# A four-layer graph network on one core: one tile fewer for ScalarE in each step's first group, and one place moved between two buffers

## The chip, the cores and the metric

The kernel runs on one core of a Trainium2 chip. A core has five engines, each with a queue of its own: TensorE (PE, with its weight loads shown as PEld), VectorE (DVE), ScalarE (ACT), GpSimd (POOL) and SyncE (SP), which here only issues transfers (DMAs). They wait for each other by semaphores. The metric is the time of one execution on the device in microseconds (us), as the median of several runs.

## The reference

The reference runs four graph layers one after the other on x (3327 x 256) with one adjacency matrix adj (3327 x 3327, about 1% of it set, plus the diagonal). Each layer normalises x, applies a ReLU and adds its result to x. What matters here is layer 0:

```python
R = S + jnp.eye(N); R = R / R.sum(-1, keepdims=True)       # S is adj
for n in range(2):                                         # two steps
    A = _top_p_attention(Xa, W1, W2, W3)
    Xf = R @ Xf
    Xa = A @ Xa
    Z = Z + Xf @ U1[n].T + Xa @ U2[n].T
```

`_top_p_attention` computes q k^T, a softmax over each row, and keeps in each row the largest probabilities until their sum reaches 0.9; the rest is set to zero and the row is divided by what was kept. Layers 1 to 3 (a sum over neighbours with tanh weights, and two attentions masked by adj) follow and are not touched.

## The kernel before

Rows are handled in 26 tiles of 128 (the last has 127). Layer 0 has two steps (s = 0 and 1), and each step handles the tiles in nine groups of three (`FG`; the last has two). All data are 32-bit floats.

**A group** (`group`, L996) goes through these stages:

- For each tile, q is loaded, PE makes the scores (L1037), DVE moves them from PSUM into the tile's buffer e with the row maxima (`evicted`, L1011), and ACT takes the exponential with the row sum (L1020). There are six buffers for e.
- A first guess of each row's threshold is made, with one DVE pass over half of each tile (L1080).
- Four rounds (`ROUNDS`, L1110) narrow the threshold. A round needs, for each tile, the sum of the entries at or above the row's threshold. DVE gets it in one pass (L1126). ACT needs two passes, a ReLU and a sign (L1121), from which DVE combines the sum (L1132, L1133). `ON_ACT` = [2, 2, 1, 2] says how many of the group's tiles ACT takes in each round; the rest are DVE's. Short DVE instructions on 128x3 values (L1136 to L1153) then move the threshold, and the next round needs the new one: ACT gets it negated (L1114).
- For each tile, DVE finds the exact cut with three passes (L1168, L1171, L1182) and appends the weighted sum to the list of other work.

**The other work** of a step, called generators in the code, is advanced beside the groups:

- `neighbours` (L898) is R @ Xf for one tile. It loads the tile's column of adj in four parts into `blk` (three places, L905). In step 0 ACT also writes the signs of each part into `sg` (L908), which go to memory for the later layers (L909). POOL adds the identity to the diagonal block (L912), after the sign was taken. PE sums 26 products in 52 matmuls in the one PSUM place of `ps_acc` (L914). ACT scales the row (`xf_row`, L922), after DVE's reciprocal of the row sum in step 0 (L920), and the row is stored (L923).
- `weighted` (L926) is A @ Xa and the update of Z for one tile. It loads the stored row into `xf_in` (L934), and in step 1 the row of Z so far into `base_row` (L932, one place). PE transposes e (L950), ACT copies it to `wt` (L952), PE sums the products (L940), and ACT scales the result (`xa` or `xa_row`, L962). Then that row and `xf_in` are transposed (L785, copied by L786) and multiplied by U1 and U2 (L970). DVE adds the row of Z (L978).

**The order of the work.** `overlapped` (L1191) starts a group every 20 ticks and advances all generators by one part each tick. This gives the program's order. Tile, the framework below it, lays down the order on each engine's queue before the run: it takes the program's order as priority and lets work go ahead whose inputs and buffers it expects to be free. So neighbour sums of later groups run ahead in the first group's rounds, before there is weighted work. Buffers come from pools: tiles with the same tag share `bufs` places, and a new tile waits until a place is free. `sg` and `xf_in` are from the pool `f0t`, whose default is two places (L1319). All transfers named here go through SP's queue.

Of the kernel before, what the change touches and what calls it, by code (L numbers as in the profile page):

```python
# [9 lines left out]
F32 = mybir.dt.float32  # L10
# [3 lines left out]
I8 = mybir.dt.int8  # L14
# [6 lines left out]
P = 128  # L21
# [4 lines left out]
D = 256  # L26
# [8 lines left out]
ON_ACT = [2, 2, 1, 2]  # L35
# [26 lines left out]
def rows_of(it):  # L62
    return P if it < NT - 1 else LAST
# [3 lines left out]
def kernel(  # L67
# [678 lines left out]
    def layers(fast):  # L746
# [9 lines left out]
        def ps_wide():  # L756
            return psf.tile([P, 2 * 512], F32, tag="wide", bufs=2, name="ps_wide")

        def ps_acc():
            return psf.tile([P, 512], F32, tag="acc", name="ps_acc0")  # L760

        def ps_out0():
            return psf.tile([P, 512], F32, tag="out", name="ps_out0")

        def ps_row():
            return psf.tile([P, 512], F32, tag="row", bufs=2, name="ps_row")
# [11 lines left out]
        def rows_to_load(it):  # L778
            return LAST_ROWS if it == NT - 1 else [(0, P)]
# [20 lines left out]
        def layer0(wp, mp, ap_, tp, sp):  # L800
            def turned(src, tag, bufs):
                t = tp.tile([P, 2, P], F32, tag=tag, bufs=bufs, name=tag)
                transposed(src, t.rearrange("p c r -> p (c r)"))
                return t
# [47 lines left out]
            def keys_of(xt, s, it):  # L852

                ps = ps_row()
                f, i = divmod(it, HB)
                for c in range(2):
                    nc.tensor.matmul(ps[:, :P], wkq[:, f, c, :], xt[:, c, :], start=(c == 0), stop=(c == 1))
                b, o = f * DA, (1 - f) * DA
                r = rows_of(it)
                nc.scalar.activation(  # L860
                    kt[b : b + DA, s, i * P : i * P + r], ps[b : b + DA, :r], AF.Copy,
                    accum_out=key_sums[b : b + DA, s, i : i + 1],
                )
                qs = tp.tile([P, P], F32, tag="qs", name="qs")
                nc.scalar.copy(qs[o : o + DA, :], ps[o : o + DA, :P])
                nc.sync.dma_start(q_d[s, it], qs[o : o + DA, :])
# [31 lines left out]
            def neighbours(s, it, xf):  # L898

                acc = ps_acc()  # L900
                w = XW if s == 0 else D
                for chunks in QB:
                    n = len(chunks)
                    blk = ap_.tile([P, 7, P], F32, tag="blk", name="blk")
                    nc.sync.dma_start(blk[:, :n, :], adj_t[it, :, chunks[0] : chunks[0] + n, :])  # L905
                    if s == 0:
                        sg = tp.tile([P, 7, P], I8, tag="sg", bufs=1, name="sg")
                        nc.scalar.activation(sg[:, :n, :], blk[:, :n, :], AF.Sign)  # L908
                        nc.sync.dma_start(sign_d[it, :, chunks[0] : chunks[0] + n, :], sg[:, :n, :])  # L909
                    if it in chunks:  # L910
                        j = it - chunks[0]
                        nc.gpsimd.tensor_tensor(blk[:, j, :], blk[:, j, :], ident, ALU.add)  # L912
                    for j, jc in enumerate(chunks):
                        nc.tensor.matmul(  # L914
                            acc[:, :w], blk[:, j, :], xf(jc)[:, :w], start=(jc == 0), stop=(jc == NT - 1)
                        )
                    yield
                yield
                if s == 0:
                    nc.vector.reciprocal(rr[:, it : it + 1], acc[:, D : D + 1])  # L920
                row = tp.tile([P, D], F32, tag="xf_row", name="xf_row")
                nc.scalar.mul(row, acc[:, :D], rr[:, it : it + 1])  # L922
                nc.sync.dma_start((xf_d, xf2_d)[s][it * P : (it + 1) * P, :], row)  # L923
                yield

            def weighted(s, it, e, norm, xa, xa_next, us):  # L926

                if s == 0:
                    base = h(it)[:, :D]
                else:  # L930
                    base = tp.tile([P, D], F32, tag="base", bufs=1, name="base_row")
                    nc.sync.dma_start(base, zz_d[it * P : (it + 1) * P, :])  # L932
                xf_in = tp.tile([P, D], F32, tag="xf_in", name="xf_in")
                nc.sync.dma_start(xf_in, (xf_d, xf2_d)[s][it * P : (it + 1) * P, :])  # L934
                po = ps_out0()[:, :D]

                def products(wt, j0, m):
                    for k in range(m):
                        jc = j0 + k
                        nc.tensor.matmul(  # L940
                            po, wt[:, k * P : (k + 1) * P], xa(jc)[:, :D], start=(jc == 0), stop=(jc == NT - 1)
                        )

                ready = None
                for j0 in range(0, NT, 8):
                    m = min(8, NT - j0)
                    pt = ps_wide()
                    for k in range(m):
                        jc = j0 + k
                        nc.tensor.transpose(pt[:, k * P : (k + 1) * P], e[:, jc * P : (jc + 1) * P], ident)  # L950
                    wt = tp.tile([P, 8 * P], F32, tag="wt", name="wt")
                    nc.scalar.copy(wt[:, : m * P], pt[:, : m * P])  # L952
                    if ready:
                        products(*ready)
                    ready = wt, j0, m
                    yield
                products(*ready)
                if s == 0:
                    row = xa_next(it)[:, :D]
                else:  # L960
                    row = tp.tile([P, D], F32, tag="xa_row", bufs=1, name="xa_row")
                nc.scalar.mul(row, po, norm)  # L962
                yield
                xt = turned(row, "xt", 2)
                xft = turned(xf_in, "xft", 2)
                yield
                pz = ps_row()
                for n, (lhs, u) in enumerate(((xft, us[0]), (xt, us[1]))):
                    for cc in range(2):
                        nc.tensor.matmul(  # L970
                            pz[:, :D], lhs[:, cc, :], u[:, cc, :],
                            start=(n == 0 and cc == 0), stop=(n == 1 and cc == 1),
                        )
                if s == 0:
                    keys_of(xt, 1, it)
                yield
                zrow = tp.tile([P, D], F32, tag="zrow", bufs=1, name="zrow")
                nc.vector.tensor_tensor(zrow, pz[:, :D], base, ALU.add)  # L978
                nc.sync.dma_start(zz_d[it * P : (it + 1) * P, :], zrow)
                yield  # L980
                if s == 0:

                    xb = tp.tile([P, D], F32, tag="xa_row", bufs=1, name="xb")
                    r = rows_of(it)
                    for a, b in rows_to_load(it):
                        nc.sync.dma_start(xb[a:b], x[it * P + a : it * P + b])
                    nc.gpsimd.tensor_tensor(xb[:r], xb[:r], b_b[:r], ALU.add)
                    nc.sync.dma_start(xb_d[it * P : it * P + r, :], xb[:r])
# [7 lines left out]
            def group(s, tiles, xa, xf, xa_next, us, slots, products_of, also):  # L996


                g = len(tiles)
# [108 lines left out]
                todo = list(products_of)  # L1108
                first = 2 if g == len(todo) else 0
                for r in range(ROUNDS):  # L1110
                    on_act = list(range(max(g - ON_ACT[r], g - 2 if g > 2 else 1), g)) if g > 1 else []
                    A = slice(on_act[0], g) if on_act else None
                    if on_act:
                        nc.scalar.mul(minus[:, 0, A], v[:, 3, A], -1.0)  # L1114
                    if r >= first and todo:
                        also.append(neighbours(s, todo.pop(0), xf))
# [74 lines left out]
            def overlapped(makers, apart, later=(), when=None):  # L1191
# [5 lines left out]
                while makers or running or also or waiting:  # L1197
# [15 lines left out]
            overlapped(  # L1213
                [
                    lambda also, t=t: group(0, t, h, h, xa1, us0, lambda it: e_slot(it % 6), t, also)
                    for t in groups
                ],
# [42 lines left out]
            def entered(it):  # L1260
# [29 lines left out]
                for c in range(2):  # L1290
# [6 lines left out]
            overlapped(  # L1297
                [
                    lambda also, t=t: group(
                        1, t, xa1, lambda jc: xf[jc // HB][:, jc % HB, :], None, us1, slots,  # L1300
                        products_of(t), also,
# [13 lines left out]
        with ExitStack() as l0:  # L1315
# [3 lines left out]
            tp = l0.enter_context(tc.tile_pool(name="f0t", bufs=2, reuse_waits="tile"))  # L1319
# [127 lines left out]
        with tc.tile_pool(name="l1", bufs=2, reuse_waits="tile") as l1:  # L1447
# [15 lines left out]
            for it in range(NT):  # L1463
# [20 lines left out]
                r = rows_of(it)  # L1484
# [244 lines left out]
```

## Time and profile before

| | us |
|---|---|
| median of 3 runs | 3117.26 |
| lowest and highest | 3114.98, 3118.21 |
| the profiled execution's own time | 3111.67 |
| its span, first to last instruction | 3109.9 |
| first x row of step 0 scaled (L962) | 216.6 |
| last of step 0 | 1016.7 |
| first x row of step 1 scaled (L962) | 1149.5 |
| last of step 1 | 1998.3 |

The mean granted TensorE clock was 0.973 of full speed. In what follows, "busy" is time in which an engine executes; a row of the stretches gives the start and end, the length, and the busy time of PE, PEld, DVE, ACT and POOL with the number of instructions, then the granted clock, the share of the DMA engines and GB/s. A row of an engine's timeline gives start, duration, engine, line, operation, output and inputs, and in brackets how long the engine was idle before it and what ended that. A row of the waits names who waited for whom, the total, the number of times and the longest. The page's group rows give the busy time, the mean duration in ns and the idle time before.

### The profile page before, as it was taken

To read this page: it belongs to the slowest core of one execution; us is meant where nothing else is said; L and a number is where in the kernel's file an instruction comes from. 1 tells how busy PE (TensorE), PEld (TensorE's weight loads), DVE (VectorE), ACT (ScalarE), POOL (GpSimd) and SP (SyncE) were. 2 spreads that over 40 slices of the span, in tenths; PEclk is the share of its full clock that TensorE was granted. 3 is DMA by queue.
4 is the path that set the end of the run, shared out by engine and by line. 5 is a ranking of instruction groups with operands and counts; after the bars stand their busy time and mean duration, and the time that the engine had idled before them with its cause. 6 is when DMAs were issued, how large, how long until landed. Compare 5 with 4: busy or idle time off the path is not lost. (4 is left out here: it accounts for less than half of the span.)

```text
span 3109.9 us, 37662 instructions
## 1 busy us (share of the span) xinstructions
PE 2831.8 (91%) x13454; PEld 2278.7 (73%) x13454; DVE 2382.5 (77%) x4159; ACT 1968.2 (63%) x2607; POOL 375.5 (12%) x716
## 2 busy tenths in 40 slices
PE   7788899999999899999999988999997999979998
PEld 5466677777778577767777767788876787758887
DVE  3678888778873588888976868577765999769996
ACT  6767787768763666677665645333334776757776
POOL 0220010000001000000000014311120233210000
PEclk9899999999999999999999999999998999989999
DMA  4431112331242232211232232388861211112221
GB/s 137 131 102 51 55 42 77 91 89 49 70 119 88 76 97 60 59 43 51 73 89 79 76 110 75 111 315 313 321 228 33 71 59 57 31 49 78 72 76 38
DMA packets 183034, 298.83 MB, mean 96 GB/s; under 512 B 24700, under 2 KB 137015, under 8 KB 179511
## 3 DMA queue, kind: packets, MB, share of 16 engines
q1 hardware_dynamic: 182838, 296.34, 30.3%
q8 instruction: 108, 1.77, 0.2%
q14 instruction: 88, 0.72, 0.1%
HBM read 251.97 MB, written 44.30 MB: 95 GB/s over the span
## 5 line engine op out<-in xcount | busy, mean ns | idle before, releaser
L1121 ACT ACTIVATE junk_a<-e,minus 128x3328 int8<-128x3328 f32 x208 | 638.7, 3071 | 3.7
L1588 PE MATMUL ps_wide<-wh,places 128*128 128x257 f32 x1872 | 452.5, 384 | 35.9 <-DVE places L1582 34.8
L1588 PEld LDWEIGHTS ps_wide<-wh,places 128*128 128x128 f32 x1872 | 354.4, 192 | 94.5 <-ACT places L1580 16.5
L914 PE MATMUL ps_acc<-h,blk 128*128 128x258 f32 x1352 | 333.6, 399 | 44.5 <-ACT xf_row L922 35.3
L1011 DVE TENSOR_SCALAR_CACHE_REDUCE e<-ps_wide 128x1024 f32<-128x1024 f32 (+1 forms) x176 | 178.4, 1019 | 212.0 <-PE ps_wide L1037 211.5
L914 PEld LDWEIGHTS ps_acc<-h,blk 128*128 128x128 f32 x1352 | 262.1, 199 | 99.9 <-ACT xf_row L922 40.5
L914 PE MATMUL ps_acc<-xf,blk 128*128 128x256 f32 x1352 | 314.0, 384 | 13.0 <-ACT xf_row L922 13.0
L940 PE MATMUL ps_out<-h,wt 128*128 128x256 f32 x1352 | 312.6, 383 | 5.0 <-ACT wt L952 4.9
L940 PE MATMUL ps_out<-xa,wt 128*128 128x256 f32 x1352 | 312.6, 381 | 1.4 <-ACT wt L952 1.4
L1579 ACT ACTIVATE places<-places,sd 128x512 f32<-128x512 f32 (+1 forms) x364 | 246.6, 685 | 105.5 <-PE ps_wide L1588 72.3
L1476 PE MATMUL ps_wide<-gw,blk 128*128 128x256 f32 x1352 | 303.9, 382 | 0.2 <-ACT blk L1473 0.2
L914 PEld LDWEIGHTS ps_acc<-xf,blk 128*128 128x128 f32 x1352 | 254.1, 191 | 63.2 <-ACT xf_row L922 18.5
L1476 PEld LDWEIGHTS ps_wide<-gw,blk 128*128 128x128 f32 x1352 | 257.0, 192 | 35.1 <-ACT blk L1473 0.6
L940 PEld LDWEIGHTS ps_out<-h,wt 128*128 128x128 f32 x1352 | 250.8, 191 | 41.1 <-ACT wt L952 7.0
L940 PEld LDWEIGHTS ps_out<-xa,wt 128*128 128x128 f32 x1352 | 248.3, 190 | 34.9 <-ACT wt L952 3.7
L1126 DVE SCALAR_TENSOR_TENSOR below<-e,v 128x3328 f32<-128x3328 f32 x72 | 265.4, 3687 | 1.8
L1580 ACT ACTIVATE places<-places,d 128x512 f32<-128x512 f32 (+1 forms) x364 | 235.9, 682 | 46.1 <-DVE places L1581 45.7
L1581 DVE TENSOR_TENSOR places<-places,places 128x1024 f32<-128x1024 f32 (+1 forms) x182 | 210.4, 1164 | 67.8 <-ACT places L1579 65.8
L952 ACT COPY wt<-ps_wide 128x1024 f32<-128x1024 f32 x208 | 175.1, 846 | 88.1 <-PE ps_wide L950 87.4
L1037 PE MATMUL ps_wide<-keys,q 64*128 64x512 f32 (+1 forms) x832 | 214.8, 567 | 16.0 <-DVE e L1011 13.1
L1582 DVE SCALAR_TENSOR_TENSOR places<-blk_s,places 128x1024 f32<-128x1024 int8 (+1 forms) x182 | 206.1, 1141 | 2.0
L1020 ACT ACTIVATE e<-e,nm 128x3327 f32<-128x3327 f32 x44 | 134.8, 3064 | 85.3 <-DVE nm L1019 85.2
(274 smaller groups left out, 4314.8 us busy)
## 6 DMA issues: line engine op xcount, KB each, us to landing
blk<-in_adj_t SPq DMA_DIRECT2D x104, 448.0 KB, 3.4
blk<-in_adj_t SPq DMA_DIRECT2D x52, 832.0 KB, 6.8
adj_rows<-in_adj SPq DMA_DIRECT2D x25, 1663.5 KB, 8.1
blk<-in_adj_t SPq DMA_DIRECT2D x104, 384.0 KB, 3.3
blk_s<-sign_d SPq DMA_DIRECT2D x72, 256.0 KB, 2.9
blk_s<-pos_d SPq DMA_DIRECT2D x44, 416.0 KB, 3.6
pos_d<-pos SPq DMA_DIRECT2D x22, 416.0 KB, 2.8
xf_d<-xf_row SPq DMA_DIRECT2D x52, 128.0 KB, 2.4
```

The source lines that it names most:

```text
L914: nc.tensor.matmul(acc[:, :w], blk[:, j, :], xf(jc)[:, :w], start=(jc == 0), stop=(jc == NT - 1))
L940: nc.tensor.matmul(po, wt[:, k * P : (k + 1) * P], xa(jc)[:, :D], start=(jc == 0), stop=(jc == NT - 1))
L1011: nc.vector.tensor_scalar(e.rearrange("p (f c) -> p f c", f=2)[:, :, c0 : c0 + cw], pl.rearrange("p (f c) -> p f c", f=2)[:, :, :cw], 1.0, ...
L1037: nc.tensor.matmul(pl[:, f * 512 : f * 512 + cw], q[f * DA : (f + 1) * DA, :], kt[f * DA : (f + 1) * DA, s, c0 : c0 + cw], start=True, sto ...
L1121: nc.scalar.activation(junk, es[i], (AF.Relu, AF.Sign)[n], bias=minus[:, 0, i : i + 1], accum_out=(ga, sa)[n][:, 0, i : i + 1],)
L1126: nc.vector.scalar_tensor_tensor(below, es[i], v[:, 3, i : i + 1], es[i], ALU.is_ge, ALU.mult, accum_out=v[:, 1, i : i + 1],)
L1476: nc.tensor.matmul(po, filt[:, j * P : (j + 1) * P], gw(jc), start=(jc == 0), stop=(jc == NT - 1))
L1579: nc.scalar.activation(e1[:, :, q, :], s0, AF.Exp, bias=sd[:, jc + q, 1:2])
L1580: nc.scalar.activation(e2[:, :, q, :], s1, AF.Exp, bias=d2[:, jc + q : jc + q + 1])
L1581: nc.vector.tensor_tensor(e1, e1, e2, ALU.max)
L1582: nc.vector.scalar_tensor_tensor(e1, signs[:, :n, j : j + 2, :], 0.0, e1, ALU.is_gt, ALU.min)
L1588: nc.tensor.matmul(pos_[k], e1[:, k, q, :], wh(jc + q)[:, : D + 1], start=(jc + q == 0), stop=(eye and jc + q == NT - 1),)
```

## The change

Three lines change, all in layer 0:

- `sg` has two places instead of one (its `bufs=1` goes, and the pool's two hold).
- `xf_in` has one place instead of two.
- In the rounds, the number of tiles for ACT is 1 for the group that begins with tile 0, in both steps, and `ON_ACT[r]` otherwise. In that group of three, rounds 0, 1 and 3 thus have one tile on ACT and two on DVE; round 2 has that already.

```diff
-                        sg = tp.tile([P, 7, P], I8, tag="sg", bufs=1, name="sg")
+                        sg = tp.tile([P, 7, P], I8, tag="sg", name="sg")
...
-                xf_in = tp.tile([P, D], F32, tag="xf_in", name="xf_in")
+                xf_in = tp.tile([P, D], F32, tag="xf_in", bufs=1, name="xf_in")
...
                 for r in range(ROUNDS):
-                    on_act = list(range(max(g - ON_ACT[r], g - 2 if g > 2 else 1), g)) if g > 1 else []
+
+                    most = 1 if tiles[0] == 0 else ON_ACT[r]
+                    on_act = list(range(max(g - most, g - 2 if g > 2 else 1), g)) if g > 1 else []
                     A = slice(on_act[0], g) if on_act else None
```

## The prediction

> **What bounds the kernel now.** I read the engine totals first, then layer 0 cut into stretches, then the queues of ScalarE (ACT) and VectorE (DVE) in the rounds that the change touches, then the waits. Totals, and the two kinds of pass over a tile that change engines:
>
> ```profile
> PE 2831.8 (91%) x13454; PEld 2278.7 (73%) x13454; DVE 2382.5 (77%) x4159; ACT 1968.2 (63%) x2607; POOL 375.5 (12%) x716
> ...
> L1121 ACT ACTIVATE junk_a<-e,minus 128x3328 int8<-128x3328 f32 x208 | 638.7, 3071 | 3.7
> ...
> L1126 DVE SCALAR_TENSOR_TENSOR below<-e,v 128x3328 f32<-128x3328 f32 x72 | 265.4, 3687 | 1.8
> ```
>
> One tile in one round costs ACT two passes of 3.07 us, 3.26 us apart with the accumulator's read (6.5 us), or DVE one pass of 3.69 us (3.77 with its read).
>
> The stretches: step 0's fill, two periods of its groups, a full period; step 1's fill and a period after it.
>
> ```profile
> 75.00:210.00 135.00, 101.62 (x404) 72.59 (x403) 93.58 (x199) 92.24 (x81) 36.94 (x46) 0.87 0.47 135
> 1025.00:1132.00 107.00, 95.20 (x411) 69.17 (x410) 74.70 (x173) 65.88 (x50) 11.22 (x23) 0.97 0.40 110
> ...
> 216.00:305.00 89.00, 78.97 (x389) 60.10 (x387) 75.70 (x147) 68.09 (x73) 2.22 (x14) 0.96 0.14 40
> 305.00:402.00 97.00, 87.71 (x424) 67.31 (x424) 84.53 (x165) 75.95 (x80) 5.58 (x19) 0.96 0.18 53
> 504.00:608.00 104.00, 98.33 (x491) 77.08 (x489) 82.40 (x159) 78.56 (x84) 3.38 (x18) 1.00 0.26 76
> 1149.00:1238.00 89.00, 82.48 (x407) 62.85 (x405) 76.85 (x149) 63.23 (x60) 4.83 (x15) 1.00 0.19 53
> ```
>
> After the length come PE, PEld, DVE, ACT and POOL busy. A full period has PE busy 98 of 104 us: TensorE (PE) bounds it. The fill has 33 us of idle PE in 135, and a clock of 0.87. The two periods behind it have 10 and 9 us idle. Step 1's fill has only 12 in 107.
>
> Why the fill is slow shows on DVE in step 0's second round, and on ACT in the same one:
>
> ```profile
> 130.74 3.69 DVE L1126 SCALAR_TENSOR_TENSOR below<-e,v 128x3328 f32<-128x3328 f32 x1
> 134.35 0.08 DVE L1126 DVE_READ_ACCUMULATOR below<-e,v 128x1 f32 x1
> 134.35 0.68 DVE L1148 SCALAR_TENSOR_TENSOR a<-v 128x3 f32<-128x3 f32 x1
> 145.80 0.16 DVE L1132 SCALAR_TENSOR_TENSOR sa<-sa,v 128x2 f32<-128x2 f32 x1 [10.77 <-ACT junk_a L1121]
> ```
>
> ```profile
> 131.04 3.07 ACT L1121 ACTIVATE junk_a<-e,minus 128x3328 int8<-128x3328 f32 x1
> ...
> 134.10 0.93 ACT L908 ACTIVATE sg<-blk 128x896 int8<-128x896 f32 x1
> 134.94 3.05 ACT L1121 ACTIVATE junk_a<-e,minus 128x3328 int8<-128x3328 f32 x1
> ```
>
> DVE does its one tile, then waits 10.77 us while ACT does four passes with signs between them.
>
> **What the Trainium skill says.** Its page "TensorE: Matmul & The Clock Gate", section Specifications, says ScalarE and VectorE run strict queues. The trace agrees: the sign at 134.10 begins only where the pass of 131.04 ends. The same page ("Part 1: The HAM clock gate") says that idle windows throttle PE: the granted clock in the fill, by stretches of 15 us, is 0.66 (150 to 165) to 1.00. The Trainium skill's page "SBUF — State Buffer", section "SBUF: two separate sides", says a DVE instruction with two SBUF inputs and a reading GpSimd (POOL) instruction exclude each other for their whole length. The trace agrees: the identity's addition to a block (L912), 0.46 us at the median, took 3.28 us at 190.48, under a DVE pass. Six more DVE passes can lengthen six such additions.
>
> **Part 1, the rounds.** Three of four rounds (0, 1, 3; round 2 already has one tile on ACT) in both steps lose one tile on ACT: 12 passes of 3.26 = 39 us of ACT work gone, 6 passes of 3.77 = 23 us of DVE work added. Per round in step 0: ACT now has 13.0 us of passes plus one to four signs of 0.9; afterwards 6.5 plus signs; DVE has 7.5 instead of 3.8, into the gap of 10.77. The round shrinks by 6.5 where ACT still ends last. Rounds 0, 1 and 3 now run from 106.5 to 130.7, 130.7 to 148.0 and 157.9 to 175.1, all ended by ACT: 3 x 6.5 = 19.5 us. In step 1 there are no signs, so DVE's 7.5 ends last: 13.0 - 7.5 = 5.5, times three is 16.5 us. Queued behind the second DVE pass are the evictions of the next group's scores (1.2 us each, for PE and the exponentials) and the reciprocal ahead of xf_row (L920), without which PE can't reuse the one ps_acc place. Each can come up to 3.8 us later; on ACT the same xf_row stands behind fewer passes. I take these as even.
>
> What of it reaches the end? PE isn't empty in these rounds: it runs the neighbour sums of later tiles ahead. One is 52 matmuls in about 11.5 us; in step 0 they come every 15 to 26 us between 115 and 190. If weighted work begins 19.5 us sooner, about one neighbour sum fewer stands behind it, and 11.5 us are owed. So step 0 gains at least 19.5 - 11.5 = 8, at most 19.5, as far as the 19 idle us of the next two periods take the debt up. I take a third of it: 12 us. In step 1 PE is idle in 12 of 107 us during the fill, so a shorter fill saves about 16.5 x 0.12 = 2 us, at most 16.5. The periods after it have only 6 to 7% idle; I take 3.
>
> **Part 2, two places for sg.** A sign now waits for the store of the one before it:
>
> ```profile
> ACT sg L908 <- DMA sign_d<-sg: 21.3, 7, 4.5
> ...
> SPq L934 <- PE ps_row L785: 139.0, 28, 17.7
> ```
>
> The first row is the fill's, the second the whole run's. Over the rest of step 0 it is another 30.9 us in 16 waits. Most delay ACT when it has nothing else. Two matter: 4.2 us at 107 in round 0, and 4.5 us at 199.8, where the copies of the first weighted tile queue behind a sign and PE idles 4.5 us. The gain is 0 to 8.7 us; some of it dies with the rounds anyway. I take 2.
>
> **Part 3, one place for xf_in.** A tile's load (L934, 2.0 us to landing) can then start only after PE has transposed the tile before (L785). It is used at the end of that tile's own products, at least 17.1 us later (the closest starts of L785 are 1000.8 and 1017.9). With two places the load already waits on this line in SP's queue, 139 us in 28 waits, because it is issued as soon as a place frees; PE's waits for a landing xf_in are nil. Behind SP's wait stand block loads and sign stores; the blocks' three places have covered that so far (PE waited once for a block, 0.8 us, in step 0's fill). base_row, which has one place in step 1, already lives so. I cost it at 2 us, between 0 and 10 for a few late ones; a gain is excluded, as a place is only taken away. If the cover is gone, a late load stops PE for about 2.5 us (issue 0.3, landing 2.0).
>
> **Sum**, against the profiled execution of 3111.7 us (span 3109.9): -12 - 3 - 2 + 2 = -15, so 3096.7. The median of the runs is 5.6 above that execution, so I expect 3102 for the median.
>
> **Rivals.**
> - *PE is the bound and only postpones* (same). The debt is paid in full: -8 - 2, no gain from sg, and xf_in costs 5: -5, 3112. For it: 98 of 104 us busy. Against it: the 19 idle us right behind the fill.
> - *The whole latency passes* (faster still). 19.5 + 16.5 + 4.5 = 40, 3077. For it: the pipeline's six tile places tie each group's scores to the weighted work two groups before, so an early start may carry on. Against it: step 1's dense PE.
> - *xf_in comes late* (slower). Place: SP's queue, where the load stands behind a block load that waits for PE to release ps_acc's operands; the longest such wait is 18.0 us, as long as the shortest spacing of the uses. Price 2.5 us for each late tile. It decides above 21 us, that is from 9 late tiles of 50: with 12, 3102 - 2 + 30 = 3130. For it: the order on the queues is fixed before the run, so a misjudged place repeats. Against it: no PE wait for it today.
>
> **Chances.** Forecast 0.47, whole latency 0.13, postponed 0.20, late xf_in 0.20. About 0.2% (6.2 us) is what a measurement of this kernel can tell from no change, so: faster 0.60, same 0.20, slower 0.20. The forecast's own range, from -6.5 to -28, is 3089 to 3111. The range over the cases, 3084 to 3125, leaves out half of the fast rival and a little over half of the slow one.
>
> **What would show it.** In the changed trace: 196 passes of L1121 instead of 208 on e (with e_h, 228 instead of 240), 94 of L1126 instead of 88; in step 0's second round a DVE wait for ACT of about 2 us instead of 10.8; the first xa row (L962) near 197 instead of 216.6, and step 1's near 1120 instead of 1149; the waits of sg for sign_d gone; no PE wait for xf_in. Step 0 should end some 12 us sooner and the rest keep its length. Wrong if the first xa row is early but step 0 ends as before (postponed), or if PE waits before L785 for a load (late).

## The result, and the profile after

| | before | changed |
|---|---|---|
| median of 8 runs each, us | 3117.74 | 3108.18 |
| lowest and highest, us | 3112.79, 3121.76 | 3102.82, 3112.04 |
| the profiled execution's own time, us | 3111.67 | 3102.82 |
| its span, us | 3109.9 | 3101.0 |
| first and last x row (L962) of step 0, us | 216.58, 1016.73 | 201.44, 1011.34 |
| first and last x row (L962) of step 1, us | 1149.46, 1998.31 | 1128.47, 1989.72 |

The changed kernel takes 0.9966 of the time of the kernel before, with a 95% interval of 0.9955 to 0.9977: 9.6 us less by the medians, 8.9 by the spans. The forecast was 15 us less, 3102 for the median. The direction and the range were right; the size was half as large again as it should have been.

From L1111 on the changed kernel's lines lie two further down: L1121, L1126, L1132 and L1168 of the kernel before are now L1123, L1128, L1134 and L1170. The page's totals and its rows for the two kinds of pass:

```profile
PE 2831.4 (91%) x13454; PEld 2280.4 (74%) x13454; DVE 2406.0 (78%) x4171; ACT 1932.2 (62%) x2583; POOL 393.2 (13%) x716
...
L1123 ACT ACTIVATE junk_a<-e,minus 128x3328 int8<-128x3328 f32 x196 | 602.0, 3071 | 4.0
...
L1128 DVE SCALAR_TENSOR_TENSOR below<-e,v 128x3328 f32<-128x3328 f32 x78 | 287.9, 3692 | 1.8
```

ACT has lost 12 passes (208 to 196) and DVE has gained six (72 to 78 on e). PE has the same work, 2831 us. The gain is therefore idle PE time that is gone, and the question is where.

DVE's timeline in the second round of step 0, where the kernel before had a wait of 10.77 us:

```profile
123.20 3.69 DVE L1128 SCALAR_TENSOR_TENSOR below<-e,v 128x3328 f32<-128x3328 f32 x1
...
127.22 3.67 DVE L1128 SCALAR_TENSOR_TENSOR below<-e,v 128x3328 f32<-128x3328 f32 x1
...
131.42 0.15 DVE L920 RECIPROCAL rr<-ps_acc 128x1 f32<-128x1 f32 x1
...
132.70 0.15 DVE L1134 SCALAR_TENSOR_TENSOR sa<-sa,v 128x1 f32<-128x1 f32 x1
```

Two passes stand where one pass and the wait stood, and the instruction that combines ACT's sum has no wait in brackets: ACT was done before it. From the first pass on e (L1126, now L1128) of round 0 to the tile stage (L1170) the first group now takes 48.05 us in step 0, from 109.01 to 157.06, and took 68.5 before: 20.5 us less. In step 1 it is 42.5 instead of 58.6: 16.1 us less.

How much of this remains shows in the stretches (columns as before). The first rows are step 0's fill and its next three periods, then step 1's fill and its next three. The periods lie between the same tiles as before. The first row can't be compared with the prediction's row of the fill, which ends 6.6 us ahead of the first x row; this one ends 1.4 us ahead:

```profile
75.00:200.00 125.00, 93.91 (x369) 65.59 (x369) 107.39 (x210) 76.97 (x70) 44.63 (x43) 0.86 0.40 121
200.00:285.00 85.00, 76.59 (x385) 58.83 (x383) 73.06 (x145) 65.23 (x71) 3.02 (x15) 0.98 0.16 45
285.00:392.00 107.00, 99.76 (x490) 77.38 (x490) 89.94 (x169) 82.41 (x86) 3.22 (x19) 1.00 0.25 72
392.00:496.00 104.00, 99.21 (x482) 77.29 (x481) 82.82 (x162) 78.45 (x84) 5.12 (x18) 0.98 0.27 77
1020.00:1111.00 91.00, 80.58 (x346) 57.01 (x347) 84.04 (x179) 46.88 (x37) 10.20 (x22) 0.96 0.38 103
1128.00:1217.00 89.00, 82.42 (x405) 62.49 (x403) 76.78 (x149) 62.89 (x59) 4.25 (x15) 1.00 0.19 51
1217.00:1315.00 98.00, 89.90 (x425) 69.04 (x426) 86.30 (x163) 69.70 (x66) 3.56 (x19) 0.95 0.20 58
1315.00:1415.00 100.00, 96.89 (x480) 76.05 (x479) 82.83 (x167) 67.14 (x64) 13.49 (x18) 1.00 0.24 70
```

Three rows of the kernel before that the prediction doesn't show: step 0's third period, and step 1's second and third.

```profile
402.00:504.00 102.00, 95.60 (x478) 74.38 (x477) 83.40 (x164) 77.38 (x84) 8.19 (x17) 1.00 0.26 76
...
1238.00:1330.00 92.00, 86.32 (x422) 65.57 (x420) 80.92 (x156) 66.28 (x62) 4.71 (x17) 1.00 0.20 56
1330.00:1423.00 93.00, 87.08 (x424) 66.25 (x424) 81.89 (x156) 66.62 (x64) 3.68 (x17) 1.00 0.19 55
```

In the changed kernel's rows, the third is the one to look at. The second period of step 0 took 97 us with PE busy 87.7 in the kernel before; now it takes 107 with PE busy 99.8 in 490 matmul records instead of 424. It holds the neighbour sum that no longer fitted into the fill. The rows scaled by `xf_row` (L922) say the same: six neighbour sums ended in the fill before (at 70, 114, 129, 155, 175 and 190 us), five now (68, 108, 132, 157 and 184). Between the x rows of tiles 3 and 6 two ended before (370 and 386), and three now (343, 364 and 384).

How much of the shorter fill was idle PE time shows from 75 us to the first x row of step 0, first before and then in the changed kernel:

```profile
75.00:216.58 141.58, 108.20 (x435) 78.32 (x434) 95.65 (x201) 98.82 (x87) 36.94 (x46) 0.88 0.45 129
```

```profile
75.00:201.44 126.44, 95.35 (x376) 66.82 (x376) 108.71 (x220) 77.06 (x70) 44.63 (x43) 0.87 0.40 120
```

The fill is 15.1 us shorter, but PE is also busy 12.9 us less in it. Only 2.3 us of what went was idle time; the rest is work that has to be done later. In the next two periods PE's idle time (length less busy time) falls from 19.3 to 15.7 us, so these take up 3.7 us of it without getting longer.

The lead of the changed kernel at successive groups' x rows in step 0 is 15.1, 20.2, 10.6, 7.8, 7.3, 7.1, 6.0 and 5.4 us, and 5.4 at the last row. The 5 us won in the first period and the 5 us lost after the second weren't traced; half of the 20.2 us goes in the second period.

In step 1 the lead is 21.0 at the first row (15.6 of it new), 21.0, 15.0, 8.1 and 8.6, and 8.6 at the last row: step 1 keeps 3.2 of its own. It pays in the same way. Five neighbour sums ended in its fill instead of six, and one in its first period instead of two. The second and third periods have three sums each, where they had two, and grew from 92 to 98 and from 93 to 100 us. Here too the shorter fill (107 to 91 us in the rows above) was nearly all PE work: PE's idle time in it fell only from 11.8 to 10.4 us.

The waits also moved. These two rows are the whole run of the kernel before, for a sign:

```profile
ACT sg L908 <- DMA blk<-in_adj_t: 57.9, 25, 8.4
...
ACT sg L908 <- DMA sign_d<-sg: 52.2, 23, 4.5
```

And in the changed kernel, with the wait of SP's queue for the place of `xf_in`:

```profile
ACT sg L908 <- DMA blk<-in_adj_t: 108.6, 40, 12.0
...
ACT sg L908 <- DMA sign_d<-sg: 4.1, 2, 2.4
...
SPq L934 <- PE ps_row L785: 189.1, 38, 22.4
```

The waits for the store of the sign before are nearly gone, 52.2 to 4.1 us, and the waits for the block itself have grown by 50.7 us. SP's waits for the place of `xf_in` grew from 139.0 to 189.1 us, yet PE never waits for a load of `xf_in`.

### The profile page after: what moved, and what is told of

The parts are those of the page before. It is cut to its first block, busy times and chain, and to the rows that moved or that the text cites. A ratio compares the mean times of both kernels' runs of the same rounds, so it can differ in the third digit from the quotient of the medians.

```text
span 3101.0 us, 37657 instructions
## 1 busy us (share of the span) xinstructions
PE 2831.4 (91%) x13454; PEld 2280.4 (74%) x13454; DVE 2406.0 (78%) x4171; ACT 1932.2 (62%) x2583; POOL 393.2 (13%) x716
## 5 line engine op out<-in xcount | busy, mean ns | idle before, releaser
L1123 ACT ACTIVATE junk_a<-e,minus 128x3328 int8<-128x3328 f32 x196 | 602.0, 3071 | 4.0
L1590 PEld LDWEIGHTS ps_wide<-wh,places 128*128 128x128 f32 x1872 | 353.8, 191 | 93.7 <-ACT places L1582 16.5
L914 PEld LDWEIGHTS ps_acc<-xf,blk 128*128 128x128 f32 x1352 | 253.9, 191 | 58.1 <-ACT xf_row L922 12.7
L1128 DVE SCALAR_TENSOR_TENSOR below<-e,v 128x3328 f32<-128x3328 f32 x78 | 287.9, 3692 | 1.8
L1037 PE MATMUL ps_wide<-keys,q 64*128 64x512 f32 (+1 forms) x832 | 215.0, 574 | 15.3 <-DVE e L1011 9.1
L1173 DVE MAX8 w<-below 128x8 f32<-128x3328 f32 x52 | 188.4, 3623 | 0.4
```

The costliest lines, as they stand in the source:

```text
L914: nc.tensor.matmul(acc[:, :w], blk[:, j, :], xf(jc)[:, :w], start=(jc == 0), stop=(jc == NT - 1))
L1037: nc.tensor.matmul(pl[:, f * 512 : f * 512 + cw], q[f * DA : (f + 1) * DA, :], kt[f * DA : (f + 1) * DA, s, c0 : c0 + cw], start=True, sto ...
L1123: nc.scalar.activation(junk, es[i], (AF.Relu, AF.Sign)[n], bias=minus[:, 0, i : i + 1], accum_out=(ga, sa)[n][:, 0, i : i + 1],)
L1128: nc.vector.scalar_tensor_tensor(below, es[i], v[:, 3, i : i + 1], es[i], ALU.is_ge, ALU.mult, accum_out=v[:, 1, i : i + 1],)
L1173: nc.vector.max(w9[:, i, 1:9], below)
L1590: nc.tensor.matmul(pos_[k], e1[:, k, q, :], wh(jc + q)[:, : D + 1], start=(jc + q == 0), stop=(eye and jc + q == NT - 1),)
```

## The experiments

The theory under test (A): the shorter rounds are a true head start, but PE had used the old, long fill to run neighbour sums ahead. A shorter fill holds one of them less, and that one is paid later, in a period that PE already fills. Against it stand: that the places of `sg` bring or cost something (sg, xf_in), that the start is lost for another reason than PE's load, and that late blocks in the fill, behind other transfers, decide. The leads below come from one profiled execution each; two kernels that should be alike there differ by up to 3 us. The last row of step 0 is at 1016.73 us before, and at 1015.63 and 1014.76 with changed places alone; it is at 1011.34 in the changed kernel, and at 1014.20 in one that differs from it in step 1 only. So smaller differences are not read, and the 3.2 us that step 1 keeps above are themselves no larger than this.

**Which part carries it.** Four kernels on one chip, with the kernel before at 3115.14 us.

The rounds alone, with the places as before:

```diff
-                    on_act = list(range(max(g - ON_ACT[r], g - 2 if g > 2 else 1), g)) if g > 1 else []
+                    on_act = list(range(max(g - (1 if tiles[0] == 0 else ON_ACT[r]), g - 2 if g > 2 else 1), g)) if g > 1 else []
```

> Only the rounds are changed (one tile on ACT in the first group of both steps); sg keeps one place and xf_in two. Theory A (the rounds carry the gain): first xa row of step 0 near 202 to 206, of step 1 some 19 us earlier than before, and 6 to 10 us less at the end (ratio 0.997 to 0.998). Rival B (the gain comes from the second place of sg, which unties ACT from the stores): ratio 0.999 to 1.001 here.

Measured: 3107.63 us, a ratio of 0.9971 (0.9960 to 0.9981), 7.5 us less. The rounds carry the gain; the lead at the first x row is 16.6 us (the row is at 199.9, earlier than expected) and at the last row of step 0 it is 3.3.

Both places alone, with the rounds as before:

```diff
-                        sg = tp.tile([P, 7, P], I8, tag="sg", bufs=1, name="sg")
+                        sg = tp.tile([P, 7, P], I8, tag="sg", name="sg")
...
-                xf_in = tp.tile([P, D], F32, tag="xf_in", name="xf_in")
+                xf_in = tp.tile([P, D], F32, tag="xf_in", bufs=1, name="xf_in")
```

> Only the buffers are changed (sg two places, xf_in one); the rounds are those of before. Theory A: within 3 us of before (ratio 0.999 to 1.001), first xa row of step 0 at 212 to 217. Rival B: 7 to 10 us less (0.997 to 0.998).

Measured: 3113.06 us, 0.9996 (0.9988 to 1.0004): no difference. The first x row came at 219.8 us, not at 212 to 217, so that part of the expectation failed. The waits of this kernel, whole run:

```profile
ACT sg L908 <- DMA blk<-in_adj_t: 92.1, 44, 6.9
...
ACT sg L908 <- DMA sign_d<-sg: 1.7, 1, 1.7
```

Without any change in the rounds, the store's 52.2 us of waits fell to 1.7 and the block load's rose from 57.9 to 92.1. A second place for the result only let ACT arrive sooner at an operand that wasn't there.

One place for `xf_in` alone:

```diff
-                xf_in = tp.tile([P, D], F32, tag="xf_in", name="xf_in")
+                xf_in = tp.tile([P, D], F32, tag="xf_in", bufs=1, name="xf_in")
```

> Only xf_in has one place; sg keeps one. Theory A: no PE wait for a load of xf_in and a ratio of 0.999 to 1.001. Rival C (the single place costs, and hides a larger gain of the other parts): 3 to 8 us more (1.001 to 1.0025), with PE idle before L785 for a load.

Measured: 3112.79 us, 0.9993 (0.9985 to 1.0001). Taking the place away costs nothing, and in this kernel too PE has no wait for a load of `xf_in`. The slow rival is refuted. Since both places together give 0.9996, the second place for `sg` is worth nothing measurable either. It was not tried alone.

The changed kernel with the new rounds in step 0 only:

```diff
-                    most = 1 if tiles[0] == 0 else ON_ACT[r]
+                    most = 1 if tiles[0] == 0 and s == 0 else ON_ACT[r]
```

> As the changed kernel, but in step 1 the first group keeps ON_ACT. Theory A: step 0 as in the changed kernel (its last xa row near 1011), step 1 as before, so 5 to 6 us less than before (ratio 0.998). If step 1 carried most of the gain instead: 1 to 2 us less (0.9995).

Measured: 3109.56 us, 0.9983 (0.9972 to 0.9993), 5.6 us less, as theory A expected. By the medians, step 0 brings a little over half of the 9.6 us and step 1 the rest; the intervals of this kernel and the changed one overlap, so the split is rough. The profiled execution, 3 us above this kernel's median, shows less: 2.5 us of lead at the last row of step 0 (at 1014.20, not near 1011) and 0.7 at that of step 1 (1997.65 against 1998.31).

The payback is the same in both kernels with new rounds above. From 75 us to the first x row the fill is 16.6 us shorter with the rounds alone and 13.9 with step 0 only, and PE is busy 16.0 and 16.8 us less in it. Five sums ended there instead of six, the second period has three instead of two, and takes 106.4 and 107.2 us instead of 97.4.

**Is it PE's load?** If PE's debt eats the head start, PE with slack must let it through. In both kernels 12 of the 26 products of each neighbour sum are left out (every second one but the last, so the sums are not the reference's):

```diff
                     for j, jc in enumerate(chunks):
+                        if jc % 2 and jc != NT - 1:
+                            continue
```

> The kernel before with 14 of the 26 products of each neighbour sum (the odd ones but the last are left out, in both steps), so PE has some 5 us less per sum, about 270 us in all; loads, signs and everything else stay. It serves as the base for the next run. Both theories: clearly faster than before, by 100 us or more (ratio below 0.97), with DVE and latency the bound in place of PE.

> The changed kernel with the same 12 products of each neighbour sum left out. Theory A (the head start of the first group is paid back because PE postpones neighbour sums and is full afterwards): with a PE that isn't full the head start survives to the end of each step, so this run is 20 to 35 us below the halved kernel of before. Rival D (the head start dies for another reason, the six places of e or DVE): it is 5 to 12 us below, as with full sums.

Measured, with the kernel before at 3113.79 us: 2997.88 (0.9631, 0.9617 to 0.9645) and 2969.61 (0.9538, 0.9525 to 0.9551). The change is now worth 28.3 us, three times as much. In step 1 the theory holds in full: 17.8 us gained at the first x row and 17.9 at the last. Eight sums ended in its fill instead of ten, and the other two came in the sixth period, which took 91.7 us with three sums in it and 93.7 with one in the kernel before: where PE had room, they cost nothing. In step 0 the theory doesn't hold: the lead is 14.4 at the first row, 11.5 at tile 12, 4.1 three tiles later and -0.7 at the end. The stretch in which it goes, first in the halved kernel before:

```profile
584.00:677.00 93.00, 82.31 (x388) 61.00 (x387) 80.62 (x158) 74.34 (x79) 4.60 (x17) 0.94 0.21 61
677.00:775.00 98.00, 82.23 (x395) 61.58 (x395) 85.69 (x166) 78.00 (x82) 3.24 (x19) 0.93 0.22 63
```

and then in the halved changed kernel, one period shifted:

```profile
480.00:573.00 93.00, 80.73 (x389) 61.18 (x388) 80.77 (x158) 74.66 (x79) 6.28 (x17) 0.94 0.20 61
573.00:673.00 100.00, 82.90 (x404) 62.07 (x403) 85.69 (x165) 77.94 (x81) 6.40 (x19) 0.95 0.23 68
```

The period of 100 us has three neighbour sums, as has that of 98 us in the kernel before, one period later; those of 93 us have two. So a third sum costs 5 to 7 us even where PE is busy only 83 of 100 us. In step 0 the postponed sum has a price that isn't PE's busy time: PE's idle time in the period in which the lead goes grew from 10.7 to 17.1 us. DVE and ACT are at 86 and 78 of 100 us there, and which of the three ends a period wasn't separated. A sum of step 0 also has four signs on ACT, 0.83 to 0.96 us each, which those of step 1 lack; leaving them out wasn't tried. The verdict is mixed. PE's load explains step 1; in step 0 nothing of the head start was left with half the sums either, so PE's load alone doesn't explain it there. Nor are the 28.3 us head start alone: of the 22.0 us between the two profiled executions 17.2 stand at the last row of step 1, and the rest came after it and is not explained.

**The transfers in the fill.** The changed kernel's first x row came at 201.4 us, not at 197, although the rounds shrank by more than predicted. The start phase's last key came 2.3 us later (75.5 instead of 73.2), and some 3 us went in the tile stage. Its timeline across the engines:

```profile
157.06 3.69 DVE L1170 SCALAR_TENSOR_TENSOR below<-e,v 128x3328 f32<-128x3328 f32 x1
...
158.23 3.11 POOL L987 TENSOR_TENSOR xb<-xb,b_b 128x256 f32<-128x256 f32 x1 [5.27 <-DMA xb<-in_x]
...
161.36 0.33 SPq L988 DMA_DIRECT2D xb_d<-xb  x1
...
167.02 0.32 SPq L988 DMA_DIRECT2D xb_d<-xb  x1
...
169.19 0.38 SPq L905 DMA_DIRECT2D blk<-in_adj_t  x1
...
172.43 0.84 ACT L908 ACTIVATE sg<-blk 128x768 int8<-128x768 f32 x1 [11.98 <-DMA blk<-in_adj_t]
```

ACT stands 11.98 us at a sign whose block is requested at 169.19 us. Ahead of that request in SP's queue stand the loads and stores of `xb`, a side product: x with a bias added, for the last addition of the kernel, one tile at a time in one place. Each store waits for POOL's addition, which runs late under DVE's passes. So here an unrelated store holds a block back, and a block holds ACT. A late block reached a round as well. In round 3 the new threshold was there at 144.5 us, but a sign stood ahead of it on ACT, and DVE then waited for ACT's passes:

```profile
147.21 0.84 ACT L908 ACTIVATE sg<-blk 128x768 int8<-128x768 f32 x1 [6.07 <-DMA blk<-in_adj_t]
...
155.26 0.16 DVE L1134 SCALAR_TENSOR_TENSOR sa<-sa,v 128x1 f32<-128x1 f32 x1 [3.29 <-ACT junk_a L1123]
```

The next kernels leave this side work out, before and after the change (so a term of the final sum is missing, and the last step reads x itself):

```diff
-                if s == 0:
+                if False:
                     xb = tp.tile([P, D], F32, tag="xa_row", bufs=1, name="xb")
...
-                    nc.sync.dma_start(xs_(it)[a:b], xb_d[it * P + a : it * P + b])
+                    nc.sync.dma_start(xs_(it)[a:b], x[it * P + a : it * P + b])
```

> The kernel before without the side work xb (x plus ln_b by POOL, written to memory, 26 loads, additions and stores in step 0's fill); x is read directly later, so ln_b is left out. Base for the next run. Theory E (SP's queue, held by xb's stores that wait for POOL, which waits for DVE's passes, delays blocks in the fill): 0 to 5 us less than before.

> The changed kernel without xb. Theory E: ACT's waits for blocks in step 0's fill fall from 28.9 us to under 10, the first xa row comes near 192 instead of 201.4, and at the end it is 12 to 20 us below the kernel before (ratio 0.994 to 0.996). Rival (the late blocks cost nothing at the end): as the changed kernel, 0.9966.

Measured, on the same chip: 3102.34 (0.9964, 0.9950 to 0.9978) and 3088.45 (0.9921, 0.9907 to 0.9934). I had expected at most 5 us for the kernel before and it is 11.4; the side work alone costs more than the whole change brings. For the second kernel I had expected 12 to 20 us and it is 25.3, so in the changed kernel the side work costs about 16 (25.3 less the change's own 9.6, which was measured apart). The first x row came at 207.1 and 183.6 us, the second earlier than the 192 us expected. But the loss in the later period is there as well, in the kernel before without the side work,

```profile
296.00:393.00 97.00, 87.47 (x426) 66.78 (x424) 84.60 (x165) 76.29 (x80) 5.74 (x19) 0.98 0.18 54
```

and in the changed one without it:

```profile
272.00:380.00 108.00, 95.96 (x464) 73.34 (x463) 92.12 (x182) 82.65 (x87) 5.46 (x20) 0.97 0.21 64
```

97 us became 108, as 97 became 107 with the side work. So the queue of transfers explains microseconds of the fill, and not the payback. ACT's waits for blocks in this fill fell from 28.9 to 14.9 us, where I had expected under 10.

Doing the side work in another place seemed a version that could beat the changed kernel. The start phase already holds x in `h`, so its rows need no second load:

```diff
             for span in spans:
                 n = len(span)
                 mv = sp.tile([P, 4, 2], F32, tag="mv0", name="mv0")
+                xb = tp.tile([P, 4, D], F32, tag="wt", name="xb")
+                for k, it in enumerate(span):
+                    r = rows_of(it)
+                    nc.gpsimd.tensor_tensor(xb[:r, k, :], h(it)[:r, :D], b_b[:r], ALU.add)
+                    nc.sync.dma_start(xb_d[it * P : it * P + r, :], xb[:r, k, :])
```

(with the load of `b_b` ahead of it and the old block removed), on top of the kernel before and of the changed one:

> The kernel before with xb made from the rows of x that the first 60 us load anyway (26 additions by POOL and 26 stores there, through the buffer wt, which is idle then); the 26 extra loads are gone and the whole reference is computed. If the start hides it: as without xb, 9 to 13 us below before (ratio 0.996 to 0.997). If it lengthens the start, where PE is busy: 0 to 6 us below.

> The changed kernel with xb made in the start. If the start hides it: 21 to 27 us below the kernel before (ratio 0.9915 to 0.993), faster than both kernels. If not: 10 to 16 us below (0.995 to 0.997).

Measured, with the kernel before at 3115.62 us: 3115.30 (1.0002, 0.9994 to 1.0011) and 3114.26 (0.9994, 0.9985 to 1.0003). The first is 0.3 us below, at the edge of the case in which the start gets longer; the second is 1.4 us below, outside both cases. The start phase is 9 to 13 us longer (its last key at 86.1 and 84.5 us instead of 73.2 and 75.5): the side work was as dear there. And the second kernel lost the change's gain too: it led its partner by 24 us at the first x row, and at the last row of step 0 it was 4.5 us behind. Only four neighbour sums ended in its fill, where its partner had five. But 15 of the 24 us go in the first period, with two sums in both kernels, and there PE's idle time grew from 5.0 to 15.2 us: most of that is no debt of PE work, and its cause stays open. No kernel faster than the changed one, with all the work in it, came of this.

**One unit of debt.** If one postponed neighbour sum is what the head start pays, making one such sum nearly free should give that back. In both kernels 18 of the 26 products of tile 5's sum in step 0 are left out:

```diff
                     for j, jc in enumerate(chunks):
+                        if s == 0 and it == 5 and jc % 4 and jc != NT - 1:
+                            continue
```

> The kernel before with 18 of the 26 products of one neighbour sum left out: tile 5's in step 0, some 8 us of PE work. It is the sixth sum, which runs here at 175 to 190 in the fill. Theory A: PE has idle time there, so 0 to 4 us less than before.

> The changed kernel with the same 18 products left out. Theory A: here the sixth sum is the postponed one, in full periods, so its 8 us return: 5 to 9 us below the changed kernel, 14 to 19 us below the kernel before (ratio 0.994 to 0.9955). Rival D (what eats the head start isn't this sum): as much as in the kernel before, 0 to 4 us below the changed kernel (0.9955 to 0.9967).

Measured, against the same kernel before at 3115.62 us: 3110.35 (0.9984, 0.9977 to 0.9991) and 3097.64 (0.9945, 0.9931 to 0.9959). By the ratios the changed kernel gains some 6.5 us by it (0.9945 against 0.9966, measured apart, with intervals that just overlap), inside the 5 to 9 that the theory asked for. But the kernel before gains 5.3, and I had expected at most 4. The change is thus worth 12.7 us instead of 9.6, and 3 us are not separated by these intervals. In the profiles the pair is 10.6 us apart at the last row of step 0 (1012.70 and 1002.14), and the full pair 5.4. But the second period is still longer. This kernel before has one sum ending in it,

```profile
309.00:399.00 90.00, 79.94 (x390) 60.22 (x390) 77.02 (x150) 68.04 (x71) 2.21 (x14) 0.98 0.14 43
```

and this changed one has two,

```profile
287.00:388.00 101.00, 88.40 (x431) 67.31 (x430) 88.53 (x181) 77.75 (x84) 3.23 (x19) 0.97 0.19 55
```

so it takes 11 us more, with PE busy 8.5 us more. So a full sum is still postponed into this period. What came back came in the third period: at the rows of tiles 0, 3, 6 and 9 the lead of this pair is 15.3, 21.7, 11.5 and 14.3 us, that of the full pair 15.1, 20.2, 10.6 and 7.8. The third period has three full sums in each of the four kernels, so this is not the price of the postponed sum, and the test doesn't decide for the theory.

## Why the prediction was right in sign and too large

- **The rounds** (predicted 19.5 and 16.5 us) measured 20.5 and 16.1. In step 1 the argument held: the three rounds lost 5.3, 6.7 and 5.6 us where 5.5 was predicted. In step 0 only the total held, and that is in part luck: rounds 0, 1 and 3 lost 10.0, 6.0 and 4.7 us where 6.5 was predicted for each. Round 0 also lost an exponential of the next group (L1020, 3.1 us) from among ACT's passes; it now runs behind them. And ACT hadn't ended that round alone: DVE stood at a reciprocal (L920) that waited for PE until 128.68 us, when ACT's passes had been over for 0.9 us. In round 1 short work of DVE's own fills the time until ACT is done, so the wait predicted at about 2 us is gone. Round 3 was held by a late block. The counts came as predicted (196, and 94 with 78 of them on e).
- **The first x row** (predicted near 197) came at 201.4. The rounds started 2.5 us later, and the tile stage took 3 us longer, with late blocks in it. The prediction took what is queued behind DVE's added passes "as even" and weighed only the identity's additions for POOL. Additions to `xb` are the ones that the passes met.
- **Step 0 is the term that was off**: 12 us in the sum, 5.4 in the profile. The mechanism was named and is in the trace: six sums ended in the fill, now five. Two sizes in "at least 19.5 - 11.5 = 8" were off. The head start at the first row was 15.1 us and not 19.5, and PE's work that left the fill was 12.9 us and not 11.5, so 2.3 us were sure and not 8. The third of the debt that the idle time was to take up, some 4 us, is about what the next two periods took up, 3.7 us. It had no derivation, so that is luck; in the kernels with the rounds alone and with step 0 only it is 1.5 and 4.8 us. The later periods lost the remaining 0.6 us.
- **Step 1** (predicted 3) measured 3.2, which one profiled execution can't fix to better than 3 us. The reason given, that PE is dense there and only the idle share of the fill is saved, fits: 1.4 us of idle time went, where 2 was predicted. The halved kernels confirm it: with PE's load reduced, all 17.8 us passed. Step 1's first x row came at 1128.5 and not near 1120, because step 0 had brought less.
- **`sg`** (predicted -2) is worth nothing measurable. The prediction priced the waits for the store and not what came next: the block load ends the same wait. This term and the next cancelled in the sum, so their errors don't show in the total.
- **`xf_in`** (predicted +2) cost nothing; its ratio alone was 0.9993, up to 1.0001. The cover named (the row is used at the end of its tile's own products) was enough, though SP's wait for the place grew by 50 us.
- **The rivals.** "PE only postpones" was forecast at 3112 and is the nearest in mechanism; the measured 3108.18 lies between it and the forecast. "The whole latency passes" is what step 1 does when PE has half the neighbour work, and not otherwise. "`xf_in` comes late" didn't happen.

Open is the rest of step 0's price. That the work which left the fill comes back in the second period is seen in the changed kernel, with the rounds alone, with step 0 only and without the `xb` work; that PE's load is what makes it cost its full price there is argued and not shown. With PE relieved, a third sum in a period still cost 5 to 7 us, and moving the `xb` work turned a lead of 24 us into a lag of 4.5. The order of work on the queues is laid down anew for each kernel, and effects of 5 to 10 us from it were seen and not taken apart. That POOL's lengthened additions delay the stores is read from one timeline; the experiment removed the additions, loads and stores together, so their shares are argued and not shown.

## What to carry to other kernels

When a pipeline's fill gets shorter, count what other work was being done ahead in it. Of the 15.1 us that went from this fill 12.9 were work of the engine that bounds the kernel, and only idle time of that engine is a gain. The idle time of the periods behind it takes up some of the work that comes later, here 3.7 us of 19.3, and not all that it seems to offer. Before giving a waiting buffer a second place, look for what would end the same wait next, which here was the load of its operand. And look through a transfer queue for unrelated stores ahead of loads: leaving such side work out gained 11 to 16 us here, and moving it into the start gained nothing.

## What the runs showed of the hardware

POOL's addition of 128x256 values takes 0.73 us at the median, and under DVE's pass it took up to 4.03 us in the changed kernel (2.71 at most before):

```profile
148.28 3.69 DVE L1128 SCALAR_TENSOR_TENSOR below<-e,v 128x3328 f32<-128x3328 f32 x1
...
148.52 4.03 POOL L987 TENSOR_TENSOR xb<-xb,b_b 128x256 f32<-128x256 f32 x1 [5.04 <-DMA xb<-in_x]
```

The addition begins just after the pass and ends when the pass has ended and a little more, 3.69 + 0.73 less the 0.24 between the starts. The Trainium skill says in "SBUF — State Buffer", section "SBUF: two separate sides", that a DVE instruction with two SBUF inputs and a POOL instruction that reads hold the shared ports for their whole length, one after the other. The trace agrees to within 0.2 us. It agrees in all eleven cases of both kernels in which such an addition took over 1 us, five before and six in the changed one: each ended 0.57 to 0.59 us after the DVE pass that it fell into. What I had not expected is the reach: the 26 additions took 25.6 us of POOL's time before and 33.4 in the changed kernel, and leaving them out, with a load and a store for each, gained 11.4 us in the kernel before.

The strict queues of ScalarE and VectorE, which the prediction places in a section Specifications of the Trainium skill's page "TensorE: Matmul & The Clock Gate", stand in the table that opens that page.
